# Where batch 1's last v projections run: beside batch 0's attention or beside its own

## Chip, cores, metric

One core of a Trainium2 chip runs the whole program. The metric is the device time of one execution in microseconds (us), median of several runs.

## What is computed

One transformer block with adaptive layer norm, all in fp32: two batches of 1024 tokens, width 1024, 32 heads of 32, a gated feed-forward layer of inner width 2752.

```python
h = layernorm(x) * (1 + ca) + sa
qkv = clip(h @ Wqkv.T, -8, 8)
q, k, v = split(qkv);  q = layernorm(q);  k = layernorm(k)
scores = q @ k.T / sqrt(32) + slope_h * (pos_k - pos_q), causal
x = x + ga * (softmax(scores) @ v) @ Wout.T
h = layernorm(x) * (1 + cb) + sb
x = x + gb * ((silu(h @ Wg.T * ag) * (h @ Wu.T * au)) @ Wd.T * ad)
```

## The kernel before

**Stages.** After a prelude and batch 0's projections of q and k, the program runs two streams at once: *attention* (batch 0, then batch 1) and *dense work* (everything else that is ready). After attention come the rest of the output projection and the feed-forward layer.

**Attention.** Work is cut into groups (b, qb, k): batch b, query block qb of 512 queries, and k, one of 8 sets of four heads. The order is b, then qb, then k (`GROUPS`). A group has one unit for each block of 128 keys, jb = 0, 1, ...: 4 units for qb = 0 and 8 for qb = 1. The diagonal units are narrower: 384, 256, 128 queries. A unit is written here as b_k_qb_jb and a group as b_k_qb. In a unit, TensorE makes the scores `sc` (L743, from `cq` and `ck`), ScalarE the exponentials `p` (L1069), GpSimd the causal mask (L1073) on diagonal units, and two units later (`LAG = 2`) TensorE weighs v with p (`av`, from `cv`). Running sums of p are added on VectorE and GpSimd (L1101); the third unit of a group also holds the previous group's row sums (`ones`, L1111). PSUM has one `sc` pair alone, so the scores of a unit wait until ScalarE has read those of the unit before. Groups k = 0 and 1 cut the exponentials into pieces of 128 and 256 queries, so ScalarE needs longer there.

**Loads of attention.** `chunk` (L1031 to L1033) loads `cq`, `ck`, `cv` of a group, two groups ahead, into two buffers each, all on SyncE's (SP's) one queue. It needs `ready`: for block 0 of batch 1 its first two pairs of v, for block 1 all four.

**Dense work.** In order (`dense_work`): the last pairs of batch 0's v; batch 1's q, k and v; then the output projection (`output`) of batch 0 (four pairs) and of batch 1's first two pairs. A pair is 256 tokens. Each takes seven products (Strassen-Winograd) of 4 matmuls of 128x512 (L743, `bank<-wB,a`, `bank<-wT,a`; in the output projection `wB_o`, `wT_o` with `aoA`, `aoS`). In the projections a generator hands over after 4 matmuls, in the output projection after 2. A q or k pair also has 16 transposes (`raw`, L746) and a layer norm; a v pair has none, only the clip (L966 to L969) and two stores to DRAM (L978). When the projections are done, their pools close and the output projection's seven weights `wB_o`, `wT_o` (1024 KB each, L804 and L808) are loaded into the same SBUF, followed on SP's queue by `ga`, `xr`, `aoA` and the weights `restw` of the last feed-forward rows (L1377).

**The pace.** TensorE's order is the program's order (`pinned`). `together` interleaves the two streams by estimated slack: `a` adds up, unit by unit, half of what a unit is thought to need on ScalarE beyond its own matmuls; `d` adds up 0.9 us for each dense matmul and 0.6 us for four transposes. Dense work is taken until `d` reaches `share(a)`:

```python
def share(a):
    if a < att_us[0]:
        return LEAD + DENSE0 * a / (0.98 * att_us[0])
    return LEAD + DENSE0 + DENSE1 * max(a - att_us[0] - 8.0, 0.0) / (att_us[1] - 8.0)

for us in itertools.chain([0.0], att):
    a += us or 0.0
    while live and (more or d < share(a)):
        us = next(dense, -1.0)
        ...
        d += us
```

SP, VectorE, GpSimd and ScalarE are ordered by the framework's scheduler. SP's transfers use eight semaphores in turn: in the built program each transfer waits for the one eight places before it to have landed. When the feed-forward stage starts, nothing of attention or of dense work is left.

Of the kernel before, what the change touches and what calls it, by code (L numbers as in the profile page):

```python
# [480 lines left out]
def kernel(  # L481
# [874 lines left out]


    OUT_US = 112.0
    LEAD, DENSE0, DENSE1 = 16.0, 370.0, 136.0

    def halves(half, jb):
        return (nc.vector, nc.gpsimd)[half]
# [728 lines left out]
```

## Time and profile before

| | |
|---|---|
| median of 3 runs | 2853.81 us (2849.35 to 2857.14) |
| profiled execution | 2848.94 us, span 2846.9 us |
| batch 0's attention with dense work | 362.0 to 936.5 us of the span |
| batch 1's attention with dense work | 936.5 to 1327.6 us |
| rest of the output projection, feed-forward | 1327.6 to 2846.9 us |
| TensorE busy over the span | 2691.8 us (95%) |

Busy times are unions of an engine's instructions. The clock column of a stretch is the mean share of full TensorE speed that was granted. A fp32 matmul shows as two records in the trace: "x8" of 128x512 is four matmuls of the program.

### The profile page before, as it was taken

To read this page: it belongs to the slowest core of one execution; us is meant where nothing else is said; L and a number is where in the kernel's file an instruction comes from. 1 tells how busy PE (TensorE), PEld (TensorE's weight loads), DVE (VectorE), ACT (ScalarE), POOL (GpSimd) and SP (SyncE) were. 2 spreads that over 40 slices of the span, in tenths; PEclk is the share of its full clock that TensorE was granted. 3 is DMA by queue.
4 is the path that set the end of the run, shared out by engine and by line. 5 is a ranking of instruction groups with operands and counts; after the bars stand their busy time and mean duration, and the time that the engine had idled before them with its cause. 6 is when DMAs were issued, how large, how long until landed. Compare 5 with 4: busy or idle time off the path is not lost. (4 is left out here: it accounts for less than half of the span.)

```text
span 2846.9 us, 29933 instructions
## 1 busy us (share of the span) xinstructions
PE 2691.8 (95%) x10271; PEld 1328.0 (47%) x10271; DVE 1462.4 (51%) x2285; ACT 687.8 (24%) x1524; POOL 1296.2 (46%) x1270
## 2 busy tenths in 40 slices
PE   6999999999999888889999999999999998999998
PEld 2444433333333222223664444444444447888776
DVE  5766525566634457666644453544536355443442
ACT  1322243444344556554111010110101101000000
POOL 3312124545565665655447474455636431322352
PEclk9999999999999899999999999999999999999999
DMA  9877863766755554433687576675857668554552
GB/s 346 310 273 300 298 233 118 234 217 209 231 152 198 149 175 136 147 128 112 199 294 244 170 251 214 186 279 162 278 176 234 199 198 267 150 148 136 167 144 79
DMA packets 377573, 579.14 MB, mean 203 GB/s; under 512 B 21590, under 2 KB 278712, under 8 KB 366276
## 3 DMA queue, kind: packets, MB, share of 16 engines
q1 hardware_dynamic: 363928, 556.12, 59.9%
q10 hardware_dynamic: 13484, 21.02, 2.3%
q8 instruction: 84, 1.38, 0.2%
q14 instruction: 77, 0.63, 0.1%
HBM read 411.89 MB, written 165.17 MB: 203 GB/s over the span
## 5 line engine op out<-in xcount | busy, mean ns | idle before, releaser
L1069 ACT ACTIVATE p<-sc,kw 128x128 f32<-128x128 f32 (+3 forms) x1024 | 422.5, 515 | 356.9 <-PE sc L743 344.4
L743 PE MATMUL bank<-wT,a 128*128 128x512 f32 x768 | 356.8, 608 | 15.1 <-ACT P L961 8.5
L1101 POOL TENSOR_TENSOR p<-p,p 128x1024 f32<-128x1024 f32 (+3 forms) x128 | 262.5, 2051 | 174.0 <-PE av L743 142.0
L1101 DVE TENSOR_TENSOR p<-p,p 128x1024 f32<-128x1024 f32 (+3 forms) x192 | 250.2, 1314 | 143.2 <-POOL p L1073 85.2
L743 PE MATMUL bank<-wB,a 128*128 128x512 f32 x576 | 262.3, 601 | 1.4 <-DVE raw L968 0.9
L743 PE MATMUL sc<-cq,ck 32*128 32x512 f32 (+3 forms) x1536 | 192.7, 540 | 55.9 <-ACT p L1069 55.6
L743 PEld LDWEIGHTS bank<-wT,a 128*128 128x128 f32 x768 | 141.2, 193 | 190.7 <-issue 163.2
L1073 POOL TENSOR_SCALAR_AFFINE_SELECT p<-p 128x256 f32<-128x256 f32 x256 | 136.7, 548 | 195.6 <-ACT p L1069 192.2
L743 PE MATMUL av<-p,cv 128*32 128x512 f32 (+3 forms) x1536 | 170.7, 512 | 3.2 <-POOL p L1073 3.2
L743 PEld LDWEIGHTS bank<-wB,a 128*128 128x128 f32 x576 | 104.6, 190 | 144.3 <-issue 126.1
L743 PEld LDWEIGHTS sc<-cq,ck 32*128 32x128 f32 x1536 | 64.6, 186 | 193.6 <-ACT p L1069 108.0
L1863 PE MATMUL gy<-bt,sig 128*128 128x512 f32 x280 | 132.2, 594 | 7.0 <-DVE gX L1670 6.9
L1863 PE MATMUL uy<-bt,siu 128*128 128x512 f32 x280 | 131.6, 592 | 0.0
L1863 PE MATMUL gx<-bt,sig 128*128 128x512 f32 x280 | 131.6, 592 | 0.0
L1863 PE MATMUL ux<-bt,siu 128*128 128x512 f32 x280 | 131.6, 592 | 0.0
L743 PEld LDWEIGHTS av<-p,cv 128*32 128x32 f32 x1536 | 33.7, 109 | 122.5 <-issue 83.5
L1863 PEld LDWEIGHTS gy<-bt,sig 128*128 128x128 f32 x280 | 52.7, 190 | 76.1 <-issue 64.1
L1863 PEld LDWEIGHTS ux<-bt,siu 128*128 128x128 f32 x280 | 53.2, 190 | 67.0 <-issue 66.5
L1863 PEld LDWEIGHTS uy<-bt,siu 128*128 128x128 f32 x280 | 53.2, 190 | 67.0 <-issue 65.3
L1863 PEld LDWEIGHTS gx<-bt,sig 128*128 128x128 f32 x280 | 53.2, 190 | 67.0 <-issue 65.7
L1863 PE MATMUL ux<-bt,wuS 128*128 128x512 f32 x160 | 75.2, 592 | 0.0
L1863 PE MATMUL gx<-bt,wgS 128*128 128x512 f32 x160 | 75.2, 592 | 0.0
(415 smaller groups left out, 4459.8 us busy)
## 6 DMA issues: line engine op xcount, KB each, us to landing
bt<-bop_T SPq DMA_DIRECT2D x140, 512.0 KB
bt<-bop_B SPq DMA_DIRECT2D x99, 512.0 KB
a<-hop SPq DMA_DIRECT2D x20, 1792.0 KB
wm<-in_L_wmod_dram SPq DMA_DIRECT2D x48, 512.0 KB
wB<-in_L_attn_Wqkv_dram SPq DMA_DIRECT2D x21, 1024.0 KB
aq_S<-act_S SPq DMA_DIRECT2D x16, 1280.0 KB
qk<-qs SPq DMA_DIRECT2D x16, 1024.0 KB
act_S<-asS SPq DMA_DIRECT2D x30, 512.0 KB
```

The source lines that it names most:

```text
L743: return in_order(nc.tensor.matmul(*args, **kw_))
L1069: last_exp[0] = nc.scalar.activation(p[:, g, lo:hi], sp[:, g, lo:hi], AF.Exp, bias=kw[:, d, h_ : h_ + 1])
L1073: last_mask[0] = nc.gpsimd.affine_select(out=p[:, :, 0:P], in_=p[:, :, 0:P], pattern=[[0, 2], [1, P]], compare_op=ALU.is_ge, fill=0.0, bas ...
L1101: adders[b](half, jb).tensor_add(dst, dst, ps[half][:, :, 0:n])
L1863: nc.tensor.matmul(ps.rearrange("p (j t) -> p j t", j=NJ), ins[mat][qa][:, c2, :], bt[:, :, c2, :], start=(q in ("P1", "P2", "P5") and c2 ...
```

## The change

Two constants. The share of dense work that is due by the end of batch 0's attention falls by 48 us of the planner's estimate, and the share due during batch 1's attention rises by as much. The sum is the same.

```diff
     OUT_US = 112.0
-    LEAD, DENSE0, DENSE1 = 16.0, 370.0, 136.0
+    LEAD, DENSE0, DENSE1 = 16.0, 322.0, 184.0
```

In the built order of TensorE, 52 dense matmuls move out of batch 0's attention into batch 1's. Before, the last product of batch 1's last v pair stands in unit 0_7_1_1 and the first product of the output projection in 0_7_1_2. After, the v pair 2 ends in 1_1_0_0, v pair 3 in 1_4_0_2, and the output projection begins in 1_5_0_1. Dense work left over at the end of attention is the same in both.

## The prediction

> **What bounds the kernel now.** First the stages: busy time of each engine (PE, PEld, DVE, ACT, POOL), then clock, DMA share and GB/s, in batch 0's attention (query block 0, block 1), batch 1's (the same), and all that follows.
>
> ```profile
> core 0: us, PE busy (x) PEld busy (x) DVE busy (x) ACT busy (x) POOL busy (x), PEclk, DMA share, GB/s
> 362.00:537.90 175.90, 171.34 (x833) 64.90 (x832) 77.72 (x129) 73.54 (x184) 72.92 (x100) 0.99 0.51 171
> 537.90:936.50 398.60, 381.72 (x1724) 139.56 (x1720) 218.58 (x307) 171.96 (x401) 221.34 (x196) 0.98 0.65 214
> 936.50:1061.10 124.60, 106.44 (x673) 35.44 (x672) 59.32 (x94) 67.96 (x173) 81.11 (x99) 0.89 0.51 150
> 1061.10:1327.60 266.50, 229.56 (x1317) 72.68 (x1317) 174.97 (x244) 159.32 (x375) 160.58 (x129) 0.97 0.40 124
> 1327.60:2846.90 1519.30, 1474.58 (x4673) 867.95 (x4673) 703.49 (x1012) 129.55 (x194) 680.96 (x679) 0.99 0.63 199
> ```
>
> TensorE (PE) bounds all stages. In batch 0's attention it idles 4.6 + 16.9 = 21.5 us, in batch 1's 18.2 + 36.9 = 55.1 us, and no other engine is above 66% busy there. So there is idle time in batch 1 into which dense work could go. How much a dense matmul fills is seen in PE's order of time, in group 1_3_1:
>
> ```profile
> 1189.42 1.14 PE L743 MATMUL sc<-cq,ck 32*128 32x512 f32 x8
> 1190.49 1.07 PE L743 MATMUL av<-p,cv 128*32 128x512 f32 x8
> 1191.49 1.98 PE L743 MATMUL bank<-wT_o,aoA 128*128 128x512 f32 x4
> 1193.40 1.14 PE L743 MATMUL sc<-cq,ck 32*128 32x512 f32 x8
> 1194.48 1.06 PE L743 MATMUL av<-p,cv 128*32 128x512 f32 x8
> 1197.09 0.93 PE L743 MATMUL sc<-cq,ck 32*128 32x384 f32 x8 [1.55 <-ACT p L1069]
> ```
>
> The unit with two dense matmuls takes 1193.40 - 1189.42 = 3.98 us, the one with none 3.69 us: it waits for ScalarE. The first two matmuls of an empty unit cost 0.3 us instead of 1.9; further ones about 0.87 each (four: 5.70).
>
> Last the handover from the v projections to the output projection, PE and then SP:
>
> ```profile
> 900.12 1.06 PE L743 MATMUL bank<-p,ones 128*32 128x512 f32 x8
> 905.16 3.75 PE L743 MATMUL bank<-wB_o,aoA 128*128 128x512 f32 x4 [3.98 <-issue]
> ```
>
> ```profile
> 899.14 0.38 SPq L804 DMA_DIRECT2D wB_o<-in_L_attn_Wout_dram  x1
> ...
> 902.56 1.61 SPq L808 DMA_DIRECT2D wT_o<-wt  x3
> ...
> 908.89 2.95 SPq L1287 DMA_DIRECT2D xr<-_attn_hidden_states_dram  x2
> 913.57 6.27 SPq L1249 DMA_DIRECT2D aoA<-ao  x2
> ...
> 933.95 0.34 SPq L1031 DMA_DIRECT2D cq<-qk  x1
> ```
>
> PE waits 3.98 us for the first weight, then runs at half speed (3.75 us for what takes 1.98). The seven weights start when the last v product has ended (899.04), call it T0. SP's next transfers are held: each waits for the one eight places before it. The second `aoA` went out at 919.46, when wT1's landing let it. From 899 the queue moved 265, 418, 409, 392 GB/s in stretches of 6, 7, 7, 7 us; the 9.5 MB of weights, v, `ga` and two `xr` are through at T0 + 25.
>
> **What the Trainium skill says.** "TensorE: Matmul & The Clock Gate", part 1, gives PE half rate after an idle window of about 3.4 us and until one busy window has passed. The trace agrees: 3.75 against 1.98 us above, mean clock 0.69 in 936.5 to 953.2, where PE idles 7.0 of 16.7 us. The same page (step-by-step) says that matmuls stay in program order, only weight loads are pulled ahead; so a score matmul without data holds the dense ones behind it. "DMA: Bandwidth & Descriptors", queues, rings and completion order, says that descriptors of a ring are consumed in its order; the held-up `aoA` agrees, and a small load sent behind the weights then lands behind them.
>
> **The change, part by part.**
>
> *1. Work moved.* No instruction of compute is added. 52 matmuls leave batch 0's attention (392 to 340) and join batch 1's (132 to 184, without the 72 after its last unit). These are v pair 3 and the last product of pair 2 (32), and five products of the output's pair 0 (20), which with all that follows now come later. With a v pair go its `a` load (1792 KB), two v stores (512 KB each), 3 ScalarE copies of 0.59 us and on VectorE 3 x 0.68 + 3 x 0.57 + 0.69 = 4.4 us; ScalarE and VectorE, 58% and 60% busy in batch 1, hide these. If that cover were gone, the two readers would hold a bank for about 1.3 us a product.
>
> *2. Tally by units.* In stretches at full clock, a unit's length depends closely on its kind and its dense matmuls (0 / 2 / 4): first of a group 2.5 / 3.6 to 4.4 / 5.3; 512 wide 3.7 / 4.0 to 4.8 / 5.7; 384 wide 3.1 / 3.8 / 4.8 to 5.5; 256 wide 2.4 / 3.6 / 5.3; 128 wide 1.8 / 3.1 / 4.8; third unit, with the sums, - / 4.4 to 4.8 / 6.3 to 6.7. Group k = 0 of block 1 can't go below 5.5 (512 wide), its ScalarE time. I take these medians, kind by kind, for the units of both built orders:
>
> ```
>                      batch 0          batch 1
> empty units       11 -> 22         33 -> 25
> tally, us         554.4 -> 520.7   368.5 -> 407.3
> measured before   574.5            391.1
> ```
>
> Batch 0 gives back 33.7 us (0.65 a matmul), as projections come in fours and twice as many units now stand empty at 3.7 us. Batch 1 pays 38.8 (0.75 a matmul): 12.6 in block 0, 26.2 in block 1. Sum **+5.1 us**. Bounds: if batch 0 gave 0.87 each, -6; if batch 1 paid 0.87 each, +11. The 20.1 and 22.6 us by which measured exceeds tally are single stalls; I leave all but the handover as they are.
>
> *3. The old handover goes.* Group 0_7_1 took 47.8 us against 41.0 in the tally: **-6.8**.
>
> *4. A new handover comes.* Now T0 lies in 1_4_0_2, and block-0 groups last some 14 us, not 44. The built SP order after the weights is `ga`, two `xr`, one `ao` store, then `cq`, `ck`, `cv` of 1_6_0. Eight places before that `cq` stands wT1, so it is issued at T0 + 20 (919.46 - 899.14), and lies behind the rest of the 9.5 MB: with its own 0.5 MB at 390 GB/s it lands at T0 + 26.7. PE gets to the scores of 1_6_0_0 after 1_4_0_3 (1.8) and 1_5_0 (14.3): T0 + 16.1. Wait 10.6 us. PE stands in order, so the output matmuls behind these scores stand too; ScalarE and GpSimd wait for the scores. Then half speed for up to 6.8 us as at 905: 3 us more. The first weight is awaited 0.7 us in 1_5_0_1, since two units lie between. **+14.3**; bounds 0.7 (the loads in time) and 20. Before, the group two ahead had all of the 48 us of 0_7_1 to land in: `cq` at 933.95 for scores at 953.2.
>
> *5. Behind it.* GpSimd's multiply of aoA12 of pair 1 stands ahead of the masks of 1_6_0_1, and its load stands on SP behind two `xr` and two `restw`. I reckon it lands at T0 + 38 and the masked p is wanted at T0 + 39: 0, at worst 10.
>
> Sum: 5.1 - 6.8 + 14.3 = +12.6. On the profiled 2848.94 us that is 2861.5; the median of the runs lies 4.9 higher, so **2866 us**.
>
> **Rivals.** *The load is in time.* If the queue serves the small `cq` sooner, or PE arrives later than I reckon, part 4 is about 1 and the sum is 5.1 - 6.8 + 1 = -1: 2853 us, no change. For it: bandwidth is shared by 16 engines. Against it: the semaphore wait alone puts the issue at T0 + 20. *Idle time is filled,* the other side: 55 us of idle in batch 1 take the dense work, batch 0 gives 0.87 a matmul, its GpSimd-laden groups having no other bound: -6 in the tally, -6.8, no new wait: -13, 2841 us. It decides if emptied units of batch 0 stay under 2.5 us rather than 3.7; against it are the empty units there. *GpSimd joins the stall:* part 5 at its worst, +23, 2877 us. That the change does nothing is excluded: the built order differs.
>
> **Chances.** About 0.3% (8.6 us) is what a measurement of this kernel can tell from no change. Late load, with or without GpSimd, and more than 8.6 us: 0.60 (own range 2863 to 2882); in between: 0.26; idle time filled: 0.14. Range 2843 to 2885: from most of the filling case to a stall of 20 us with GpSimd's share.
>
> **What would show it.** Right: batch 0's attention about 40 us shorter, batch 1's about 53 longer, PE idle some 10 us before `sc` around group 1_6_0 with SP's `cq` issued 20 us after the first `wB_o`, and half clock after it. Wrong: scores of 1_6_0_0 without a wait; batch 1 longer by less than batch 0 is shorter; a new stall elsewhere, as at `bank<-ident,xr` or `bank<-ident,raw`; or a change after attention's end.

## The result: slower, by more than forecast

The changed kernel takes 2883.98 us (median of 4 runs, 2880.18 to 2886.58), the kernel before, run beside it, 2852.95 us. The ratio is 1.0107, 95% interval 1.0088 to 1.0127: 31 us slower, where 12.6 us were forecast. The profiled execution took 2880.18 us, its span 2878.4 us.

The profile after begins with the same table of stages: busy time of each engine, then clock, DMA share and GB/s, in batch 0's attention (query block 0, block 1), batch 1's (the same), and the rest.

```profile
core 0: us, PE busy (x) PEld busy (x) DVE busy (x) ACT busy (x) POOL busy (x), PEclk, DMA share, GB/s
363.90:527.30 163.40, 153.72 (x789) 58.04 (x789) 70.46 (x106) 72.62 (x183) 69.73 (x94) 0.99 0.50 172
527.30:903.00 375.70, 350.64 (x1661) 129.32 (x1661) 219.73 (x313) 169.13 (x396) 220.19 (x195) 0.99 0.60 195
903.00:1051.20 148.20, 117.65 (x689) 39.35 (x688) 46.53 (x61) 69.22 (x174) 65.47 (x88) 0.87 0.52 166
1051.20:1357.90 306.70, 267.72 (x1409) 88.51 (x1408) 208.70 (x300) 160.49 (x379) 188.17 (x148) 0.96 0.42 133
1357.90:2878.40 1520.50, 1477.69 (x4670) 870.16 (x4669) 703.91 (x1008) 129.93 (x195) 677.75 (x676) 0.99 0.63 199
```

Batch 0's attention is 574.5 - 539.1 = 35.4 us shorter, block 0 of batch 1 is 23.6 us longer (124.6 to 148.2), block 1 of batch 1 is 40.2 us longer (266.5 to 306.7). What lies before and after attention differs by 1.9 and 1.2 us. Block 1 is the new thing: its added TensorE work is 26 us by the tally, and 40 came.

The handover lies where it was expected. First PE's order of time, then SP's.

```profile
1007.28 0.85 PE L743 MATMUL av<-p,cv 128*32 128x384 f32 x8
1020.48 2.09 PE L743 MATMUL sc<-cq,ck 32*128 32x512 f32 x8 [12.35 <-DMA ck<-qk]
1022.50 2.04 PE L743 MATMUL bank<-wB_o,aoA 128*128 128x512 f32 x2
```

```profile
990.47 0.39 SPq L804 DMA_DIRECT2D wB_o<-in_L_attn_Wout_dram  x1
...
1005.54 1.05 SPq L1031 DMA_DIRECT2D cq<-qk  x1
1009.33 0.32 SPq L1032 DMA_DIRECT2D ck<-qk  x1
```

PE waits 12.35 us for the `ck` of 1_6_0, which SP issued 18.9 us after the first output weight. The clock is at half by then: the score matmuls take 2.09 us instead of 1.14, and two dense records 2.04, the usual time of four.

The second loss is in group 1_3_1, the group in which the prediction showed how a dense matmul fills an empty place. PE after, then VectorE (DVE):

```profile
1200.65 1.14 PE L743 MATMUL sc<-cq,ck 32*128 32x512 f32 x8
1201.72 1.07 PE L743 MATMUL av<-p,cv 128*32 128x512 f32 x8
1207.64 1.12 PE L746 MATMUL bank<-ident,xr 128*128 128x128 f32 x4 [4.84 <-DVE h2t L849]
```

```profile
1196.45 7.64 DVE L1101 TENSOR_TENSOR p<-p,p 128x1024 f32<-128x1024 f32 x3 [0.30 <-PE av L743]
...
1204.62 1.68 DVE L1101 TENSOR_TENSOR p<-p,p 128x1024 f32<-128x1024 f32 x1
1206.23 1.35 DVE L849 TENSOR_SCALAR h2t<-bank,modt 128x128 f32<-128x128 f32 x4
```

Four transposes of an output pair wait 4.84 us for their bank. VectorE must read the previous four transposes out of it (L849), and stands until 1206.23 in running sums of p (L1101). Three sums take 7.64 us, 2.5 each. The unit takes 8.0 us, where the tally has 3.7.

PE's waits in block 1 of batch 1, by what ended them (us in total, times, longest), before and then after:

```profile
PE sc L743 <- ACT p L1069: 27.7, 26, 2.2
PE bank L743 <- DVE h2t L849: 4.5, 1, 4.5
...
PE bank L746 <- DVE h2t L849: 0.9, 1, 0.9
```

```profile
PE bank L746 <- DVE h2t L849: 15.7, 6, 4.8
PE sc L743 <- ACT p L1069: 14.2, 14, 2.2
PE bank L746 <- DVE xr L727: 4.8, 1, 4.8
```

The added dense work halves the waits for ScalarE, as meant: 27.7 to 14.2 us. It does not shorten the stage by as much, because waits for VectorE around the transposes rise from 5.4 us (4.5 of them at a dense product that needed the bank) to 20.5. Within attention, 76 instead of 56 of VectorE's reads L849 lie in block 1: before, 16 stood in block 0, where no running sum is wider than 128x768; 48 of VectorE's 81 in block 1 are 128x1024.

### The profile page after: what moved, and what is told of

Its sections match the earlier page's. It is cut to its first block, busy times and chain, and to the rows that moved or that the text cites. A ratio compares the mean times of both kernels' runs of the same rounds, so it can differ in the third digit from the quotient of the medians.

```text
span 2878.4 us, 29934 instructions
## 1 busy us (share of the span) xinstructions
PE 2699.7 (94%) x10271; PEld 1334.5 (46%) x10271; DVE 1475.8 (51%) x2285; ACT 686.9 (24%) x1524; POOL 1301.1 (45%) x1270
## 4 chain that ended last, share of the span: by engine, by line
PE 41%; issue 3%; DVE 3%; DMA 2%; POOL 2%; SPq 1%; ACT 0%; POOLq 0%; DVEq 0%; ACTq 0%
PE gx L1863 8%; PE ux L1863 8%; PE dx L1988 7%; PE gy L1863 6%; PE uy L1863 6%; PE dy L1988 5%; DMA bop_T<-inner_T 1%; DVE asS L1817 1%; DMA actr<-rac 0%; PE dr_T L1921 0%; PE dr_C L1921 0%; POOL dX L1933 0%; POOL x_X L1934 0%; DVE inner_T L1178 0%; SPq L1184 0%
## 5 line engine op out<-in xcount | busy, mean ns | idle before, releaser
L743 PE MATMUL bank<-wT,a 128*128 128x512 f32 x768 | 362.6, 617 | 13.0 <-ACT P L961 7.9
L1101 POOL TENSOR_TENSOR p<-p,p 128x1024 f32<-128x1024 f32 (+3 forms) x128 | 264.0, 2062 | 189.4 <-PE av L743 163.6
L1101 DVE TENSOR_TENSOR p<-p,p 128x1024 f32<-128x1024 f32 (+3 forms) x192 | 247.0, 1299 | 98.5 <-POOL p L1073 60.7
L743 PEld LDWEIGHTS av<-p,cv 128*32 128x32 f32 x1536 | 33.7, 109 | 123.8 <-issue 82.7
L968 DVE TENSOR_TENSOR raw<-P,bank 128x512 f32<-128x512 f32 x48 | 32.8, 683 | 105.7 <-PE bank L743 105.6
L849 DVE TENSOR_SCALAR qs<-bank,vt 128x128 f32<-128x128 f32 x144 | 50.1, 402 | 52.1 <-PE bank L746 51.3
```

Source lines behind the costliest of these rows:

```text
L743: return in_order(nc.tensor.matmul(*args, **kw_))
L849: nc.vector.tensor_scalar(dst(k), tp[:, j, :], mul(k), add(k), ALU.mult, ALU.add)
L968: nc.vector.tensor_add(dst, part_t[MATE[q]], bank)
L1101: adders[b](half, jb).tensor_add(dst, dst, ps[half][:, :, 0:n])
```

## Experiments

Runs e1 to e16 each make one edit, to the changed kernel where nothing else is said. A ratio is to the kernel before, run on the same chip, with its 95% interval; a difference to another kernel is one of medians.

### The handover alone: e1

```diff
-                nc.sync.dma_start(qc, ...)   # and kc, vc
+                eng = nc.scalar if i == 22 else nc.sync
+                eng.dma_start(qc, ...)       # and kc, vc
```

Group 22 is 1_6_0; its three loads leave SP's queue.

> The changed kernel, with cq, ck and cv of one group (1_6_0) issued from ScalarE's queue in place of SP's, where they no longer stand behind the seven output weights. Theory (the new handover costs what the prediction says): the wait of 12.35 us of the scores of 1_6_0_0 for ck goes to under 1 us, with its half clock, and the kernel takes about 2870 us (13 to 14 less than the 2884 of the changed kernel, 17 more than before). Rival (the wait only shows there, as TensorE is ahead of something else, say VectorE): under 5 us are gained and a wait of the same size shows within two groups.

Measured 2872.19 us, ratio 1.0062 (1.0038 to 1.0085): 12 us less than the changed kernel. `ck` was issued at 990.50, 1.1 us after the first weight, and PE's wait for it is gone. The handover is worth 12 of the 31 us and no more.

### Reads by ScalarE, and later transposes: e2, e3, e5

e2 gives every second read L849 of batch 0's pairs and of batch 1's first two to ScalarE.

```diff
-    ..., lambda k: modt[:, 3, k, b : b + 1], g, False,
+    ..., lambda k: modt[:, 3, k, b : b + 1], g, b == 0 or j < NJ // 2,
```

> The changed kernel, with the evictions h2t of the output pairs within attention (L849) half on ScalarE, half on VectorE, where all were on VectorE. Theory (the further stalls in batch 1 are transposes of a finished pair that wait for VectorE, whose queue is full of attention's sums): the waits of bank<-ident,xr for h2t of 3.5 and 4.8 us go, the one for L727 stays, and 5 to 10 us are gained: about 2876 us. Rival (these stalls come from where the pairs happen to fall, or from GpSimd): no change beyond 3 us, or the waits move to another reader.

Measured 2910.36 us, ratio 1.0190 (1.0168 to 1.0212): 26 us more than the changed kernel. Now the transposes wait for ScalarE, 23.0 us in 7 waits, the longest 5.3, and the scores wait for its exponentials 36.6 us instead of 32.3. The waits moved to the other reader, as the rival had it. A fraction of busy time (52% in block 1) did not make ScalarE a free engine.

e3 puts the transposes of each output pair two products later, in both batches; e5 has e1's edit and does so for batch 0's output alone.

```diff
-        yield from output(0, range(NJ), *out_args)
+        yield from output(0, range(NJ), *out_args, 3)
...
-        yield from output(1, range(NJ // 2), *out_args)
+        yield from output(1, range(NJ // 2), *out_args, 3)
```

> The changed kernel, with the transposes of a finished output pair placed from the fourth product of the next pair on, where they were placed from the second. Theory (at the faster pace of batch 1 the layer norm between two pairs is late by a few us on VectorE): all waits of bank<-ident,xr shrink, L727's to 0, and the time is about 2870 us (some 12 gained, 2 of it by the tally of units). Rival (the single bank and VectorE's queue hold the transposes wherever they stand): the waits at h2t stay, under 5 us gained.

Measured 2879.93 us, 1.0095 (1.0076 to 1.0113). Batch 1's attention took 444.3 instead of 454.9 us, but what follows 1530.5 instead of 1520.5: batch 1's input of the feed-forward reached DRAM later, and PE waited 10.8 us for it (`rest`, `hl<-h`). The gain was handed back.

> The changed kernel with both new waits treated: cq, ck, cv of group 1_6_0 from ScalarE's queue, and the transposes of batch 0's output pairs placed from the fourth product of the next pair on (batch 1's as they were, so that their h2 reaches DRAM in time for the tail). Theory (31 us = tally 5 - old handover 5 + new handover 12 to 14 + VectorE's waits at the transposes 15, plus the rest by which half clock grew): 12 to 14 and some 7 to 10 us go; about 2862 us. Rival (a price of the move that lies in neither): 2870 us or more.

Measured 2873.30 us, 1.0083 (1.0069 to 1.0097), no better than e1. The waits at transposes went to other places (9.0 + 4.8 + 4.3 us in batch 1, against 14.4 + 4.8 in e1). At the changed pace a later place does not end these waits.

### Half the move: e4

```diff
-    LEAD, DENSE0, DENSE1 = 16.0, 322.0, 184.0
+    LEAD, DENSE0, DENSE1 = 16.0, 346.0, 160.0
```

> DENSE0, DENSE1 = 346, 160: half of the move. By the tally of units 7.4 us more than before; the handover falls in 1_1_0_1, and the scores of 1_3_0_0 come 23 us after the first output weight is issued, where ck lands 27 after: a wait of 4 us (with half clock 6). Theory (tally and handover, and stalls at VectorE that grow with the pace): about 2853 + 7.4 - 5.4 + 6 + 5 = 2866 us. Rival (a fixed price of leaving batch 0 for the output projection): nearly all of the 31 us, 2880; rival (proportional to the work moved): 2868 without a wait for ck.

Measured 2875.74 us, 1.0069 (1.0048 to 1.0091). Half of the move costs 22 of the 31 us. The late `ck` costs 6.1 us here, in 1_2_0, and waits for VectorE's L849 and L727 9.2 us in batch 1: the loss is not in proportion to the work moved.

### A finer grain of the projections: e6, e7, e11

Batch 1's projections hand over after two matmuls instead of four (a second edit keeps the small steps that go with each product at one per product).

```diff
-    todo.places(q0, n, lambda e: side(...)), KC // 2
+    todo.places(q0, n, lambda e: side(...)), KC // 4 if b else KC // 2
```

> The changed kernel, with batch 1's projections handing over after 2 matmuls in place of 4, so that no unit of batch 0's attention stands empty (22 before) and 18 in batch 1's (25). The tally of units says 919.8 against 928.0 us: 8 us gained, so about 2876 us, with TensorE's waits of sc for ScalarE (53.5 us in the two attentions) down to some 40. Rival (empty units are not what batch 0 loses by): no change beyond 3 us.

Measured 2854.39 us, 1.0007 (0.9996 to 1.0018): 30 us less than the changed kernel, far more than forecast. In the profiles, 25.7 us apart, 21.7 are in the first six groups of batch 1, 117.3 us after and 95.6 here. SP in e6:

```profile
971.82 0.32 SPq L1031 DMA_DIRECT2D cq<-qk  x1
972.19 0.42 SPq L1032 DMA_DIRECT2D ck<-qk  x1
974.48 0.38 SPq L804 DMA_DIRECT2D wB_o<-in_L_attn_Wout_dram  x1
```

Here the built order of SP has `cq` and `ck` of 1_6_0 ahead of the weights, and group 1_5_0 took 18.1 instead of 28.3 us. The groups 1_0_0 to 1_4_0 took 77.5 instead of 89.0, where the tally gave 4.8 of the 11.5. The waits at transposes stayed: 15.2 + 4.8 us. Block 1 takes 311.4 us instead of 306.7. So e6 cures block 0 and not block 1.

e7 joins e1's edit, e6's and e5's.

> The changed kernel with the finer grain, the early load of 1_6_0 and the later transposes. If the costs add, 2884 - 13 - 8 - 8 = 2855 us, level with before (2853); if the three overlap, 2862. Faster than before by over 0.3% only if the tally (3 us under that of before) and the missing old handover (5) are all that is left: 2845.

Measured 2850.18 us, 0.9992 (0.9984 to 1.0001): level with the kernel before.

e11 has the finer grain alone in the kernel before.

> The kernel before, with batch 1's projections handing over after two matmuls. Theory: the finer grain gained 30 us in the changed kernel because projections stood there in fours in batch 1's short groups, and since it also moved the chunk of 1_6_0 ahead of the output weights; before, those projections lie beside batch 0, where the tally is +4.6 us for the finer grain (559.0 against 554.4), so the time is 2850 to 2858 us. Rival: the finer grain is worth its gain wherever it is, by fewer waits for ScalarE and GpSimd: 2825 to 2840 us.

Measured 2855.90 us, 1.0018 (1.0009 to 1.0028). Nothing is gained: batch 0 grew from 574.5 to 578.1 us, close to the tally's 4.6. The finer grain pays where projections stand in batch 1's short groups (and, in e6, 4.6 us in batch 0's emptied ones), so it repairs what the change brought.

### Less work for VectorE, or for GpSimd: e9, e10, e13, e16

e9 and e10 leave out VectorE's running sums of batch 1, in the changed kernel and in the one before.

```diff
                 for half in range(2):
+                    if b == 1 and adders[b](half, jb) is nc.vector:
+                        continue
...
-            nc.vector.tensor_copy(rs, sm)
+            if b:
+                nc.vector.tensor_scalar(rs, sm, 1.0, 1e32, ALU.mult, ALU.max)
+            else:
+                nc.vector.tensor_copy(rs, sm)
...
```

> The changed kernel, with VectorE's running sums of batch 1's exponentials left out (81 instructions and 106 us of VectorE in query block 1 alone); row sums are then only GpSimd's share, raised to 1e32, so batch 1's attention output is not the reference's. TensorE's order is the same. Theory: the output pairs' transposes wait because VectorE's reads of the transpose bank stand behind these sums. Then the 20.5 us of waits of L746 in batch 1 fall under 5, half clock in batch 1 falls by 10 us or more, batch 1's attention takes 425 to 432 us instead of 455, and the time is about 2856 us, 11 to 15 above the kernel before with the same cut. Rival: the transposes wait for something else (the banks, the order on TensorE), and the cut leaves batch 1 within 5 us of 455 and the difference to the kernel before with the same cut at 25 us or more.

> The kernel before with the same cut: VectorE's running sums of batch 1's exponentials left out, row sums raised to 1e32. Theory: only 5.4 us of waits for VectorE's reads of the transpose bank stand in batch 1 here, so batch 1's attention falls from 391 to about 382 us, and the time to about 2844 us. Rival (the cut speeds all of batch 1 by shorter waits for masked exponentials and ScalarE): batch 1 falls by 20 us or more in both kernels, and the cut says nothing on the difference.

Measured 2843.74 us for the changed kernel (0.9979, 0.9971 to 0.9988) and 2842.06 for the one before (0.9967, 0.9955 to 0.9980). The 31 us between them are 1.7, where 11 to 15 were expected. Block 1 of batch 1 in e9, and PE's waits in it:

```profile
1052.60:1323.60 271.00, 255.04 (x1413) 84.04 (x1412) 106.11 (x219) 160.45 (x379) 150.43 (x147) 1.00 0.49 151
```

```profile
PE sc L743 <- ACT p L1069: 15.1, 18, 2.2
PE bank L746 <- DVE h2t L849: 0.8, 2, 0.5
```

The transposes' waits are 0.8 instead of 20.5 us and the clock of the stage is full (the changed kernel has 23.9 us at half clock there by the clock records, e9 none). The stage is 35.7 us shorter: 23.0 of idle time (39.0 to 16.0) and 12.7 of PE's busy time (267.7 to 255.0), which is half clock that no longer follows the waits. In the kernel before, the same cut takes 4.6 us from block 1 (266.5 to 261.9). So the loss in block 1 needs VectorE's sums, or what they do to GpSimd, which is 150 instead of 188 us busy there in e9.

The handover stays in e9 (11.0 us idle in 1_5_0_3), yet the two kernels are level. Without the sums the work moved into block 1 costs 271.0 - 261.9 = 9.1 us there, where the tally has 26.4.

Is it the amount of VectorE's own work? e13 hands some of it over: in batch 1, GpSimd takes half of the sums instead of a quarter.

```diff
-    together(attention(apools, (halves, mostly), banks), dense_work(), share)
+    together(attention(apools, (halves, halves), banks), dense_work(), share)
```

> The changed kernel with GpSimd taking half of batch 1's running sums instead of a quarter: in query block 1 some 24 instructions leave VectorE (31 of its 106 us of sums) and cost GpSimd about 53 us (2.2 us each), which then is busy some 240 of 300 us. The output is the reference's. Theory (VectorE's backlog in front of the transposes is the cause): waits of L746 in batch 1 fall from 20.5 to about 10 us and batch 1's attention from 455 to about 440 us, 2869 us; if GpSimd's masks come late, some of it comes back as waits of av for masked exponentials. Rival (what helped in the cut was less work for both engines and their exchange, not VectorE's backlog): GpSimd becomes the bound of block 1, batch 1 stays at 450 us or more, 2880 us or more.

Measured 2901.87 us, 1.0187 (1.0168 to 1.0206): 18 us more than the changed kernel, so the theory in that form falls and the rival's number holds. VectorE had fewer sums, and PE waited for it at the transposes 17.4 + 5.9 us, 2.8 more than without the edit. More came from GpSimd, busy 231.9 of 322.8 us in block 1: PE's waits for masked exponentials there rose from 3.9 to 11.2 us. With them half clock rose from 23.9 to 47.8 us. e16 does the reverse: GpSimd's quarter is left out, VectorE keeps its whole list (the edit of e9 with `is nc.gpsimd`).

> The changed kernel with GpSimd's quarter of batch 1's running sums left out (33 instructions and 74 us of GpSimd in query block 1); VectorE keeps all its own 81, row sums are raised to 1e32, so batch 1's attention output is not the reference's. TensorE's order is the same. Theory, formed after e13: VectorE and GpSimd hold each other up, since a 128x1024 sum of VectorE takes about 1.2 us alone and 2.5 beside a sum of GpSimd. Then VectorE's mean sum of 128x1024 falls from 1572 ns to under 1300, the waits of L746 in batch 1 from 20.5 to 5 to 10 us, and batch 1's attention from 455 to about 435 us: 2860 us. Rival (the number of VectorE's own sums in front of the transposes sets the waits): they stay at 15 us or more and batch 1 at 448 us or more.

Measured 2852.99 us, 1.0009 (1.0000 to 1.0019). PE's waits for VectorE in block 1 are now these, against 15.7 and 4.8:

```profile
PE bank L746 <- DVE h2t L849: 6.3, 5, 3.3
PE bank L746 <- DVE xr L727: 0.5, 1, 0.5
```

Batch 1's attention takes 424.5 instead of 454.9 us, 30 less, where 20 were expected; the waits fell as forecast, the mean wide sum less than expected, to 1427 ns. VectorE's sums of 128x1024 in block 1 (count, busy us, mean ns, idle before them), after, e13, e16:

```profile
L1101 DVE TENSOR_TENSOR p<-p,p 128x1024 f32<-128x1024 f32 x48 | 74.3, 1572 | 9.8 <-POOL p L1101 5.7 <-POOL p L1073 2.9 <-PE av L743 1.0
```

```profile
L1101 DVE TENSOR_TENSOR p<-p,p 128x1024 f32<-128x1024 f32 x32 | 65.6, 2049 | 6.5 <-POOL p L1073 4.1 <-PE av L743 1.8
```

```profile
L1103 DVE TENSOR_TENSOR p<-p,p 128x1024 f32<-128x1024 f32 x48 | 67.1, 1427 | 1.7 <-PE av L743 1.0 <-POOL p L1073 0.6
```

In these three, the more GpSimd has to add, the longer VectorE's same instruction takes: 2049, 1572, 1427 ns. A third fewer wide sums saved VectorE only 8.7 us in e13. The kernel before has 1635 ns in its block 1, so the change did not bring this slowness: it brought more transposes and reads beside it. The idle time is no simple measure, because in both kernels GpSimd and VectorE add by turns to the same running sum (GpSimd at odd jb of one half); e13 and e16 end that exchange as well, and with it the 5.7 us.

GpSimd's sums are not its whole share. In group 1_3_1, in the place shown above, e16 shortened the wait from 4.84 to 3.27 us only, and three sums still took 6.54 us: GpSimd spends 4.3 us of that time on additions for the output pair (`xr`, `aoA`). How one engine holds the other is seen in the changed kernel in group 1_7_1, VectorE and then GpSimd (POOL):

```profile
1333.79 1.22 DVE L1101 TENSOR_TENSOR p<-p,p 128x1024 f32<-128x1024 f32 x1
1334.92 2.32 DVE L724 TENSOR_SCALAR fix_f<-fix_f 128x2 f32<-128x2 f32 x1
1337.24 1.23 DVE L1101 TENSOR_TENSOR p<-p,p 128x1024 f32<-128x1024 f32 x1
```

```profile
1333.91 3.30 POOL L1101 TENSOR_TENSOR p<-p,p 128x1024 f32<-128x1024 f32 x1 [7.33 <-PE av L743]
```

GpSimd's sum starts 0.1 us after VectorE's and takes 3.30 us. VectorE's next instruction, two numbers a partition and 0.17 us at other places, ends only when GpSimd's sum does, 2.32 us later. They take turns, and GpSimd waits too: its 128x1024 sums in block 1 take 2.92 us in the mean in the changed kernel and 2.37 in e9. The Trainium skill, "SBUF — State Buffer", section "SBUF: two separate sides", has this as a rule: VectorE and GpSimd share a pair of ports under an exclusive lock, held for a whole instruction. Its rule names VectorE instructions with two SBUF inputs, as the sums have, or in a two-port mode; L724 has one input, so by that rule it ran in such a mode, which no record here shows. "Perfetto Trace Analysis", section "Optimizing Scalar/DVE Operations", warns that moving operations between the two might not help. e13 agrees: it lost 18 us, though of the idle time that it added the later masks had the larger part (7.3 us, against 2.8 at the transposes).

### A version that beats both: e8, e12, e14, e15

e8 is the kernel before with batch 0's output transposes two products later.

> The kernel before, with the transposes of batch 0's output pairs from the fourth product on. Its waits of TensorE for VectorE at the output's transposes are 5.4 us. Theory (the changed kernel has three times as much of this wait, as pairs follow one another faster): at most 5 us gained, 2848 to 2853 us. Rival (the later place is better by itself, whatever the pace): 8 us or more gained, as in the changed kernel.

Measured 2842.23 us, 0.9969 (0.9957 to 0.9981): 9.4 us faster than the kernel before, run beside it, and the fastest complete version here. Batch 1's attention falls from 391.1 to 384.4 us, and PE's waits for `h2t` in it from 5.4 to 1.9 us. The theory allowed 5 us at most: the later place is better at the old pace, and it paid less in the changed kernel (e3 4 us, e5 nothing beside e1).

> The kernel before with both, batch 1's projections handing over after two matmuls and batch 0's output transposes put two products later. Theory: the gains don't meet at any place, so this stands to the kernel with the later transposes alone (2842.2 us) as the finer grain alone stands to before: 2840 to 2848 us. Rival: 2820 to 2832 us, the best of all, if the finer grain pays in batch 0 too.

Measured 2848.47 us, 0.9990 (0.9980 to 0.9999). The finer grain on top of e8 loses what it loses alone.

> The changed kernel with the finer grain, the early chunk of 1_6_0 and batch 0's output transposes two products later, and with GpSimd taking half of batch 1's running sums. Theory: e7's 49.1 us of idle time in batch 1, half of it behind VectorE, falls by 8 to 12 us: 2835 to 2842 us against 2850.2, faster than the kernel before. Rival (GpSimd becomes the bound): 2850 us or more.

Measured 2862.25 us, 1.0044 (1.0029 to 1.0059), 12 us more than e7.

> The kernel before with batch 0's output transposes two products later and GpSimd taking half of batch 1's running sums. Theory: with only 1.9 us of waits for VectorE left at the transposes in batch 1, relieving VectorE gains nothing here: 2840 to 2846 us against 2842.2. Rival: GpSimd's longer list delays masks and operands of the output projection: 2850 us or more.

Measured 2845.20 us, 0.9981 (0.9973 to 0.9989), level with e8 as far as these runs tell. So moving sums to GpSimd cost 18 and 12 us at the changed pace and some 3 at the old one, where PE's waits for masked exponentials rose as well, from 3.4 to 8.9 us. Why the old pace bears this better was not tried by itself.

## Why the prediction was wrong in size

**Direction and range held; the size did not.** Forecast +12.6 us, measured +31 (31.5 between the two spans). That the range held is luck: 2884 us lies 1 us under its upper end, which stood for a stall of 20 us at the handover with GpSimd's share, and neither came. The case that did come, a late load, had a range of its own, 2863 to 2882.

**The work moved (part 2): right.** For batch 0 the forecast was 33.7 + 6.8 = 40.5 us shorter, and 35.4 were measured. The old handover went: group 0_7_1 exceeds its tally by 1.4 instead of 6.8 us. Where the missing 5 us went is not shown: in batch 0 PE's waits for ScalarE rose from 9.3 to 21.2 us (the tally has part of these, as empty units), those for VectorE's layer norm `raw` from 8.0 to 11.7, those for masked exponentials from 0 to 1.6.

**The new handover (part 4): right in mechanism, and in size by luck, as wrong terms balance.** The forecast was 10.6 us of wait and 14.3 in all. Measured: 12.35 us of wait, and groups 1_5_0 and 1_6_0 together 15.4 above their tally; e1 gives back 12. `cq` went out 15.1 us after T0, not 20; the data came 30.0 after it, not 26.7; PE arrived at 17.7, not 16.1. Block 0 of batch 1 should have cost 12.6 + 14.3 = 26.9 us and cost 23.6. That `ck` was late because of the weights ahead of it is shown by e1 and, unplanned, by e6. The prediction took the held-up `aoA` as a sign that a ring keeps its order; by its own account SP held that load back until wT1 had landed, so it says nothing on the ring. e1 gave `ck` another queue and an earlier issue at once; which of the two counted was not separated.

**GpSimd's masks (part 5): right at 0.** PE's waits for masked exponentials are 3.9 us in batch 1, against 3.2 before.

**The step that failed** is the last sentence of part 2: "single stalls; I leave all but the handover as they are". In block 1 the excess over the tally rose from 10.8 us (266.5 - 255.7) to 24.6 (306.7 - 282.1), by 13.8 of the 18.9 us that were missed; batch 0's 5.1 is the next largest, batch 1's block 0 came out 3.3 better, and 3.1 lie before and after attention, where the prediction had nothing. Part 1 held that ScalarE and VectorE "hide these", being 58% and 60% busy; it spoke of a v pair's reads alone, and for the output's 20 further reads in block 1 it had no term. VectorE's share in block 1 hardly moved, 175.0/266.5 = 66% before and 208.7/306.7 = 68% after. What counted was what stands ahead of a read in VectorE's order at the moment at which TensorE needs it. The prediction listed "a new stall elsewhere, as at `bank<-ident,xr`" among the signs of its failure, and this is that stall: L746 waits 20.5 us where reads cost 5.4 before, with half clock after the longer ones (by the clock records 61.4 us of half clock in batch 1, against 41.0).

**The rival "idle time is filled"** was wrong in outcome. Its mechanism is there: waits for ScalarE halved in block 1, and without VectorE's sums (e9, e10) the moved work costs only 9.1 us in block 1. The waits that the filling removed were replaced by waits on VectorE; e9 shows that these need VectorE's sums, and e16 that most of them need GpSimd's beside them.

**Open.** How much of VectorE's delay is longer instructions and how much is waiting for GpSimd's masks and sums was not separated: e16 changes both, the mean of a wide sum by 48 x 0.145 = 7.0 us, the idle time before those sums by 8.1. The edit of e16 was not made in the kernel before, so it is not shown how much of its 31 us would be gained there too. Nor was the direct remedy tried, the reads L849 ahead of the sums in VectorE's order. Also, e6's gain in groups 1_0_0 to 1_4_0 is 6.7 us above its tally, without an experiment of its own.

## What to carry to other kernels

When work is moved to fill idle time, ask at each place what it brings along for the other engines, each with its list in a fixed order, and which of TensorE's next instructions waits at the end of such a list; a stage's busy share of 68% hid 20 us of such waits. A small load that shares a queue with megabytes of weights is better issued ahead of them: here a way around them was worth 12 us. Before moving vector work between VectorE and GpSimd, look whether the same instruction takes longer while the other runs, and what else waits for the engine that gets the work; here taking sums away from either engine helped the changed kernel by 31 to 40 us, and moving them cost 18.

## What the runs showed of the hardware

- A sum of 128x1024 fp32 on VectorE took 1.22 us where nothing held it, 2.5 in the stretch shown, and 1.43 us in the mean of block 1 without GpSimd's sums (e16), 1.57 with a quarter of them on GpSimd (1.64 in the kernel before), 2.05 with half (e13).
- A VectorE instruction of 128x2, 0.17 us elsewhere, ended 2.32 us after its start while GpSimd was in a 128x1024 sum; GpSimd's own sums of that size took 2.92 us in the mean beside VectorE's and 2.37 without them (e9).
- VectorE's reads L849 of the PSUM bank took 0.40 us each: 398, 399, 399 and 404 ns in before, after, e13 and e16. They are late, not slow.
- Of 35.7 us that block 1 gained in e9, 23.0 were idle time and 12.7 half clock that followed the stalls: here a stall cost about half as much again as its idle time.
